# A four-layer convolution net on one core: new order numbers for the first layer, and half of the last tile's sums on another engine

## The chip, the cores and the metric

The kernel runs on one core of a Trainium2 chip, as one program. The metric is the device time in microseconds from the start of the program to its end on that core. The core's engines are TensorE (PE in the profile, its weight loads PEld), VectorE (DVE), ScalarE (ACT), GpSimd (POOL) and SyncE (SP, which here only issues transfers). Each takes its own instructions strictly in order and waits on semaphores for the others. Everything is computed in float32.

## The reference

Four layers are applied to x of shape 8 x 16 x 256 x 256. Each adds to x a function of the group-normalised x. The change lies in the first, a convolution with capsule routing over the eight images:

```python
votes = conv(gn(x), w)            # 3x3, 16 -> 128 channels = 8 atoms x 16
logits = 0
for _ in range(3):
    r = softmax(logits, axis=0)   # over the 8 images
    preds = squash(sum_over_atoms(votes * r))
    logits = logits + sum_over_channels(votes * preds)
x = x + preds
```

The other layers are a spline convolution, an attention over patches and a circular convolution. The change does not touch them.

## The kernel before

The first layer (`layer0`) works in 64 tiles of four image rows, `TILES = H // 4`. For one tile `work(i)` writes down the steps; none is emitted there. Each step is one call of `op` with its engine, an estimated time, a function that emits its instructions, and what it reads and writes. In the order of the list they are:

- `prepare` for the tile two further on: the load of the input (L478, SP), products L487 that take the mean out (PE), the move L490 (ACT), and the store L499 to a DRAM buffer (ACT queue).
- The votes, in two halves of two rows. The first half takes for each row one set of loads L528 (SP), eight small products L557 and eight L550 (PE) and two copies L572 into the votes buffer (ACT). The second half takes loads L610 and products L587 and L591 with copies L596.
- A squash: squares L641 (ACT), norm products L645 (PE), roots L659 to L661 (ACT), L665 and L666 (DVE), inverses L670 and L671 (ACT), L675 to L678 (POOL).
- Two rounds. Each has the factor products L697 (PE), a scaling L715 and two multiplications L723 (DVE) and the products L733 (PE) for each half; the copy L755 or L766 (ACT) and in the second round the sum L760 (POOL); the softmax over the images: transposes L780 (PE), maximum and difference L786 and L787 (DVE), exponential L792 (ACT), sum, reciprocal and share L796 to L798 (DVE), transposes back L804 (PE), copy L813 (ACT); and the weighted sum (`weighted`): products L831 (PE), products with the votes L842 (DVE, four for each half, into `dd` buffers) and five sums L851 (POOL) for each half. A squash follows.
- The end: factors L697 (PE), scalings L893 (DVE), the addition of x L896 (POOL, with the residual loaded by L884, SP), statistics L908 (ACT), and the stores L919 to L928 (SP).

`_Order` turns the list into one order for all engines. Each step has one number in the module's list `TIMES`, by its place counted from the end of the tile's list, and the step's rank is that number plus 48 for each tile:

```python
for m, o in enumerate(reversed(ops), 1):
    at = n * self.period + self.times[-m] if n else -1000.0 - m
    o.rank = (at, n, -m)
```

A heap then emits the step of smallest rank among those whose feeding steps have been emitted and for whose new buffers there is room. A step of a small or negative number is so emitted as soon as what feeds it has been. The buffers are counted by kind: `x=3` PSUM pairs (used by L487, the votes, the factors and the L831 of pairs of images), `u=2` PSUM banks, `v=6` votes, `dd=4` products, `io=1` for the input of L487 and the residual in turn, `pr=2` for L723. Several tiles are in work at once, their steps mixed on each engine, and the order in the steady part repeats from tile to tile.

Of the kernel before, what the change touches and what calls it, by code (L numbers as in the profile page):

```python
# [12 lines left out]
ALU = mybir.AluOpType  # L13
# [10 lines left out]
TILES = H // 4  # L24
# [160 lines left out]
class _Buf:  # L185
# [10 lines left out]


TIMES = [
    -1017.19, 743.46, 708.62, 498.18, -984.65, -996.51, -997.22, 751.01, 751.99, 751.01, 752.12, 750.77,
    -967.35, -903.62, -974.59, 753.99, 754.00, 753.77, 445.66, 393.73, -780.66, -960.80, 755.37, 755.59, 760.20,  # L200
    707.64, 775.69, 780.13, 782.25, 565.91, 658.76, 763.54, 681.24, 605.08, 709.84, 767.15, 644.09, 776.33,
    664.78, 790.04, 756.59, 796.59, 757.08, 765.74, 797.09, 318.31, 799.87, 800.80, 377.30, 696.72, 800.88,
    717.59, 571.56, 737.04, 802.63, 604.46, 530.71, 804.53, 784.88, 636.95, 657.50, 800.06, 517.07, 807.24,
    715.03, 742.15, 830.33, 840.65, 809.85, 812.29, 605.85, 802.98, 816.03, 807.95, 821.83, 824.88, 831.28,
    830.39, 840.66, 789.85, 845.72, 805.49, 748.11, 612.37, 736.06, 636.75, 809.44, 848.88, 838.39, 852.49,
    854.69, 850.98, 859.07, 855.18, 468.16, 857.49, 859.83, 859.02, 698.63, 610.89, 868.22, 704.59, 653.78,
    580.88, 884.00, 654.67, 695.12, 888.80, 889.83, 889.82, 808.47, 890.27, 690.66, 805.44, 696.48, 782.31,
    896.59, 899.53, 896.48, 777.07, 667.15, 682.59, 886.03, 640.00, 674.37, 898.75, 899.76, 887.82, 843.57,
    670.73, 902.64, 828.29, 828.95, 658.08, 885.55, 571.52, 801.95, -872.70, 907.37, 403.39, 814.67, 908.69,
    735.69, 919.60, 844.76, 829.08, -789.01  # L210
]


# [79 lines left out]
class _Net:  # L293
# [123 lines left out]
    def layer0(self, wd, bd, less0, tiles=range(TILES)):  # L417
# [5 lines left out]
        nc, tc = self.nc, self.tc  # L423
        xf = self.d["x"].rearrange("b c h w -> (b c) (h w)")
        last = B - 1
        with ExitStack() as st:
# [23 lines left out]
            for row in (0, H + 1):  # L450
                nc.sync.dma_start(
                    out=self.d0[row * ROW : row * ROW + ROW].rearrange("(p w) -> p w", p=P), in_=ring[0][:, 0, :]
                )
                nc.sync.dma_start(
                    out=self.x1[row and 15, :, :, row and 9, row and 1, :].rearrange("b c w -> (b c) w"),
# [3 lines left out]
                    out=self.x1p[:, row and 1, :, row and H // 2, :], in_=ring[0][:, 0, 0:W]  # L459
# [7 lines left out]
            def buf(kind, shape, name=None):  # L467
                pool = psum if kind in banks else sbuf
                n = {**places, **banks}[kind]
                return _Buf(kind, lambda: pool.tile(shape, F32, name=name or kind, tag=kind, bufs=n))  # L470
# [34 lines left out]
            def work(i):  # L505
# [3 lines left out]
                def op(*a, **k):  # L509
                    ops.append(order.op(*a, **k))  # L510
# [109 lines left out]
                def voted(h, a):  # L620
                    return [(v[h], a // 4, 0), (v[h], a // 4, 1)]
# [8 lines left out]
                def rows(ap):  # L630
                    return ap.rearrange("p (r w) -> p r w", w=W)
# [184 lines left out]
                def weighted(rs):  # L816


                    s = buf("s", [P, 2, 2, W])
                    for h in range(2):  # L820

                        def term(images, h=h):

                            rb = [buf("x", [P, 2, 512], "rb") if len(a) == 2 else buf("u", [P, 1, 512], "r6") for a in images]

                            def products():
                                for pair, r in zip(images, rb):
                                    for n, a in enumerate(pair):
                                        g, j = a // 4, (0, 2, 1, 3)[a % 4]
                                        at = slice(32 * j, 32 * j + 32)  # L830
                                        nc.tensor.matmul(  # L831
                                            r()[:, n], spread[at, g, h, :], rs()[at], start=True, stop=True
                                        )

                            op("PE", 1.25, products, [(rs, 0)], [(r, 0) for r in rb] + [(s, "turn")], mode="r32")
                            out = []
                            for pair, r in zip(images, rb):
                                n, a = len(pair), pair[0]
                                dd = buf("dd", [P, 2, 512])

                                def multiply(n=n, a=a, r=r, dd=dd):
                                    nc.vector.scalar_tensor_tensor(  # L842
                                        dd()[:, :n], r()[:, :n], 1.0 / B, v[h]()[:, a : a + n], ALU.subtract, ALU.mult
                                    )

                                op("DVE", 0.2 + 0.52 * n, multiply, [(r, 0)] + voted(h, a), [(dd, 0)])
                                out.append(dd)
                            return out

                        def add(out, a, b, us):  # L850
                            op("POOL", us, lambda: nc.gpsimd.tensor_tensor(out[0](), a[0](), b[0](), ALU.add),  # L851
                               a[1] + b[1], out[1])

                        d45, d6 = term([(4, 5), (6,)])
                        sh = (lambda h=h: s()[:, :, h], [(s, h)])
                        add(
                            sh,
                            (lambda h=h: rows(v[h]()[:, last]), voted(h, last)),
                            (lambda d=d6: rows(d()[:, 0]), [(d6, 0)]),
                            1.3,  # L860
                        )
                        d01, d23 = term([(0, 1), (2, 3)])
                        both = (d01, [(d01, 0)])
                        add(both, both, (d45, [(d45, 0)]), 2.4)
                        add(both, both, (d23, [(d23, 0)]), 2.4)
                        for n in range(2):
                            add(sh, sh, (lambda d=d01, n=n: rows(d()[:, n]), [(d01, 0)]), 1.3)
                    return s
# [941 lines left out]
```

## Time and profile before

| | us |
|---|---|
| median of 3 runs | 6244.17 |
| lowest, highest | 6235.46, 6245.69 |
| profiled execution | 6237.4 |
| its span, first to last instruction | 6235.3 |
| TensorE busy | 5930.8 (95%) |
| VectorE busy | 4895.1 (79%) |
| GpSimd busy | 3593.7 (58%) |
| ScalarE busy | 3073.6 (49%) |

The profile is of one execution. Its page gives each engine's busy time, the span in 40 equal slices of 156 us (a digit is the busy share in tenths), and groups of instructions by source line; the trace behind it answers by stretch of time, by wait and in order of time. L851 is line 851 of the kernel. A count such as x8 is of instructions on the chip, where a float32 product takes two. Times of matmuls overlap by a little, so that the distance from one start to the next is what counts.

### The profile page before, as it was taken

How to read it: one execution, taken by the hardware profiler on the slowest of the kernel's cores; microseconds unless marked ns; L12 is line 12 of the kernel's file. 1: busy time of each engine (PE TensorE's matmuls, PEld its weight loads, DVE VectorE, ACT ScalarE, POOL GpSimd, SP SyncE). 2: the span in 40 equal slices, each digit the busy share in tenths (PEclk: the TensorE clock that was granted, in tenths of full speed). 3: DMA queues.
4: the chain of work that ended last, by engine and by line, in shares of the span. 5: the costliest groups of instructions: out<-in, count | busy, mean ns of one | idle time of the engine just before them, and what ended most of it. 6: DMA issues, size and time to landing. Idle time of an engine off the chain costs nothing.

```text
span 6235.3 us, 111335 instructions
## 1 busy us (share of the span) xinstructions
PE 5930.8 (95%) x44488; PEld 2760.5 (44%) x44488; DVE 4895.1 (79%) x5771; ACT 3073.6 (49%) x4858; POOL 3593.7 (58%) x3040
## 2 busy tenths in 40 slices
PE   2999999999999999999968999999999999999998
PEld 0344444444444444444423444444444666666652
DVE  5799999999999999999968999999999433333321
ACT  0444544444454445444427888888888222111221
POOL 0588888888888888888873333434443111111123
PEclk9999999999999999999978999999999999999999
DMA  7455555555555555555516555555557443444358
GB/s 286 120 137 126 144 140 134 132 144 137 130 139 142 136 126 146 138 133 133 129 40 194 177 175 176 179 175 173 175 177 191 116 90 85 89 94 103 87 183 255
DMA packets 408790, 902.08 MB, mean 145 GB/s; under 512 B 62034, under 2 KB 195762, under 8 KB 364882
## 3 DMA queue, kind: packets, MB, share of 16 engines
q1 hardware_dynamic: 364434, 831.69, 48.8%
q10 hardware_dynamic: 33984, 34.08, 1.7%
q0 software_dynamic: 9856, 29.20, 1.7%
q8 instruction: 351, 5.75, 0.4%
q14 instruction: 165, 1.35, 0.1%
HBM read 684.09 MB, written 210.77 MB: 144 GB/s over the span
## 4 chain that ended last, share of the span: by engine, by line
PE 59%; DVE 26%; issue 7%; DMA 4%; POOL 3%; ACT 1%; SPq 0%; DVEq 0%; POOLq 0%; ACTq 0%
PE rb L831 8%; PE cv L587 7%; PE pqk L1535 7%; DVE bases L1089 7%; PE pl L733 6%; DVE e L1079 4%; PE cv L591 4%; PE po L1562 4%; PE cv L550 4%; PE pv L1542 4%; PE psc L1550 4%; PE p L1627 3%; DVE pr L723 2%; DVE a L1079 2%; DVE e L1058 2%
## 5 line engine op out<-in xcount | busy, mean ns | idle before, releaser
L1112 PE MATMUL ps<-bases,tw 128*32 128x512 f32 (+1 forms) x13824 | 1360.1, 546 | 16.5 <-POOL bases L1081 6.5
L851 POOL TENSOR_TENSOR dd<-dd 128x1024 f32<-128x1024 f32 x512 | 1210.9, 2365 | 70.9 <-DVE dd L842 65.6
L1081 POOL TENSOR_TENSOR bases<-e,a 128x1024 f32<-128x1024 f32 (+1 forms) x264 | 621.1, 2375 | 925.6 <-DVE e L1079 925.6
L723 DVE TENSOR_TENSOR pr<-v,fb 128x2048 f32<-128x2048 f32 (+1 forms) x512 | 1020.8, 2014 | 17.1 <-PE pl L733 12.6
L1112 PEld LDWEIGHTS ps<-bases,tw 128*32 128x32 f32 x13824 | 597.7, 109 | 800.3 <-issue 483.3
L842 DVE SCALAR_TENSOR_TENSOR dd<-rb,v 128x1024 f32<-128x1024 f32 x768 | 906.5, 1214 | 8.9 <-POOL dd L851 3.3
L851 POOL TENSOR_TENSOR s<-s,dd 128x512 f32<-128x512 f32 x512 | 647.0, 1274 | 15.1
L831 PE MATMUL rb<-rs,ct_fold 32*128 32x512 f32 x3072 | 592.9, 634 | 25.6 <-DVE pr L723 20.2
L1546 ACT ACTIVATE vt<-pv,w_b2v 128x128 f32<-128x128 f32 x512 | 146.1, 368 | 839.6 <-PE pv L1542 839.6
L733 PE MATMUL pl<-pr,ct_fold 128*32 128x512 f32 x3584 | 506.9, 603 | 4.3 <-DVE pr L723 4.3
L587 PE MATMUL cv<-kt,w 128*128 128x512 f32 x1024 | 497.2, 608 | 11.0 <-DMA kt<-d 9.8
L851 POOL TENSOR_TENSOR s<-v,dd 128x512 f32<-128x512 f32 x256 | 328.6, 1283 | 292.5 <-DVE dd L842 292.5
L1535 PE MATMUL pqk<-w_qk,t 128*128 128x512 f32 x1024 | 482.7, 594 | 4.6 <-POOL t L1529 4.6
L550 PE MATMUL cv<-kt,w 128*128 128x512 f32 x1024 | 477.4, 609 | 2.5 <-DMA kt<-d 2.5
L1567 DVE TENSOR_TENSOR y<-po,res 128x512 f32<-128x512 f32 x128 | 88.5, 691 | 490.1 <-PE po L1562 476.0
L1529 POOL TENSOR_TENSOR t<-t,emb 128x512 f32<-128x512 f32 x128 | 162.1, 1267 | 515.8 <-DVE t L1525 501.4
L1089 DVE SCALAR_TENSOR_TENSOR bases<-xr,xm,bases 128x1024 f32<-128x1024 f32 (+1 forms) x264 | 446.5, 1729 | 0.3 <-POOL bases L1081 0.3
L596 ACT COPY v<-cv 128x1024 f32<-128x1024 f32 x256 | 251.8, 1007 | 303.1 <-PE cv L591 303.1
L1066 ACT ACTIVATE sq<-a 128x1024 f32<-128x1024 f32 (+1 forms) x264 | 263.8, 999 | 230.2 <-DVE a L1058 229.5
L831 PEld LDWEIGHTS rb<-rs,ct_fold 32*128 32x128 f32 x3072 | 226.1, 185 | 325.5 <-issue 129.3
L697 PEld LDWEIGHTS fb<-f,ct_fold 64*128 64x128 f32 x3072 | 208.7, 188 | 310.5 <-issue 177.0
L842 DVE SCALAR_TENSOR_TENSOR dd<-r,v 128x512 f32<-128x512 f32 x256 | 176.9, 691 | 190.8 <-PE r L831 176.3
(281 smaller groups left out, 10164.7 us busy)
## 6 DMA issues: line engine op xcount, KB each, us to landing
xr<-x1p SPq DMA_DIRECT2D x120, 1024.0 KB
kt<-d SPq DMA_DIRECT2D x256, 387.0 KB
kt<-d SPq DMA_DIRECT2D x128, 516.0 KB
d<-dn ACTq DMA_DIRECT2D x64, 516.0 KB
kr<-d SPq DMA_DIRECT2D x128, 258.0 KB
kt<-d SPq DMA_DIRECT2D x128, 258.0 KB
x<-y SPq DMA_DIRECT2D x128, 258.0 KB
xs<-in_x_dram SPq DMA_DIRECT2D x16, 2048.0 KB
```

The source lines that it names most:

```text
L550: nc.tensor.matmul(ps[g]()[:, n], w[:, 0], t[:, a : a + 2, 0:W], start=False, stop=True)
L587: nc.tensor.matmul(ps()[:, n], w2[:, 0, j, :], t[:, a : a + 2, 0:W], start=True, stop=False)
L723: nc.vector.tensor_tensor(pr()[:, :n].rearrange("p n (r w) -> p n r w", w=W), v[h]()[:, 4 * g : 4 * g + n].rearrange("p n (r w) -> p n r w ...
L733: nc.tensor.matmul(pl()[at : at + 32], sel[:, g, h, :], pr()[:, t, :], start=h == 0 and g == 0, stop=h == 1 and (g == 1 or t == 3),)
L831: nc.tensor.matmul(r()[:, n], spread[at, g, h, :], rs()[at], start=True, stop=True)
L842: nc.vector.scalar_tensor_tensor(dd()[:, :n], r()[:, :n], 1.0 / B, v[h]()[:, a : a + n], ALU.subtract, ALU.mult)
L851: op("POOL", us, lambda: nc.gpsimd.tensor_tensor(out[0](), a[0](), b[0](), ALU.add), a[1] + b[1], out[1])
L1079: nc.vector.tensor_tensor(q, q, part[4 + k], ALU.mult)
L1081: nc.gpsimd.tensor_tensor(ring[n % 3][:, 0, p : p + m, 1 : 1 + W], rows(e), rows(a), ALU.subtract)
L1089: nc.vector.scalar_tensor_tensor(r, rows(part[1]), xm[:, b : b + 1], v, ALU.is_gt, ALU.mult)
L1112: nc.tensor.matmul(out if k is None else out[:, k], lhs, rhs, start=start, stop=stop, skip_group_check=True)
L1535: nc.tensor.matmul(ps, t[:, n, k * P : (k + 1) * P], wqk[:, n, :], start=n == 0, stop=n == 1)
```

## The change

All 149 numbers of `TIMES` are replaced. The period of 48, the lists of steps, their buffers and what feeds what stay. Besides, in `weighted`, the function `add` takes its engine from outside: for the second half (`h` = 1) of the last tile (`i` = 63) the five sums of each round go to VectorE, `nc.vector.tensor_tensor` in place of `nc.gpsimd.tensor_tensor`. All others stay on GpSimd.

```diff
--- before.py
+++ after.py
@@ -196,18 +196,19 @@
 
 
 TIMES = [
-    -1017.19, 743.46, 708.62, 498.18, -984.65, -996.51, -997.22, 751.01, 751.99, 751.01, 752.12, 750.77,
-    -967.35, -903.62, -974.59, 753.99, 754.00, 753.77, 445.66, 393.73, -780.66, -960.80, 755.37, 755.59, 760.20,
-    707.64, 775.69, 780.13, 782.25, 565.91, 658.76, 763.54, 681.24, 605.08, 709.84, 767.15, 644.09, 776.33,
-    664.78, 790.04, 756.59, 796.59, 757.08, 765.74, 797.09, 318.31, 799.87, 800.80, 377.30, 696.72, 800.88,
-    717.59, 571.56, 737.04, 802.63, 604.46, 530.71, 804.53, 784.88, 636.95, 657.50, 800.06, 517.07, 807.24,
-    715.03, 742.15, 830.33, 840.65, 809.85, 812.29, 605.85, 802.98, 816.03, 807.95, 821.83, 824.88, 831.28,
-    830.39, 840.66, 789.85, 845.72, 805.49, 748.11, 612.37, 736.06, 636.75, 809.44, 848.88, 838.39, 852.49,
-    854.69, 850.98, 859.07, 855.18, 468.16, 857.49, 859.83, 859.02, 698.63, 610.89, 868.22, 704.59, 653.78,
-    580.88, 884.00, 654.67, 695.12, 888.80, 889.83, 889.82, 808.47, 890.27, 690.66, 805.44, 696.48, 782.31,
-    896.59, 899.53, 896.48, 777.07, 667.15, 682.59, 886.03, 640.00, 674.37, 898.75, 899.76, 887.82, 843.57,
-    670.73, 902.64, 828.29, 828.95, 658.08, 885.55, 571.52, 801.95, -872.70, 907.37, 403.39, 814.67, 908.69,
-    735.69, 919.60, 844.76, 829.08, -789.01
+    -241.80, 1267.36, 967.15, 1267.78, -317.12, -9592.42, -9510.80, 1237.73, 1244.26, 1244.40, 1189.33, 1179.12,
+    -411.35, -9592.40, -9565.99, 1247.56, 1247.54, 1247.55, 1127.18, 1050.73, -9570.40, -9417.31, 1249.49,
+    1225.65, 1258.37, 1194.66, 1272.62, 1204.40, 1275.43, 1128.46, 1155.43, 1267.32, 1155.75, 1186.63, 1134.96,
+    1158.05, 1252.16, 1272.85, 1257.73, 1047.50, 1282.74, 1285.57, 1285.59, 1287.82, 1291.47, 905.73, 1252.61,
+    1294.01, 1292.82, 1234.61, 1144.78, 1295.16, 837.55, 1072.04, 1247.71, 1296.90, 882.08, 1298.35, 1301.08,
+    1301.07, 1278.03, 1113.28, 1302.33, 1303.94, 1270.90, 1045.97, 1272.85, 1321.07, 1312.22, 1013.34, 949.41,
+    1101.94, 1187.26, 1069.24, 1228.20, 1319.61, 1321.06, 1286.61, 1324.53, 978.08, 1335.17, 1245.21, 1301.69,
+    1009.77, 1336.18, 1182.73, 1240.39, 1342.35, 1262.73, 1347.48, 1290.73, 1343.30, 1359.45, 1350.46, 973.22,
+    1353.21, 1290.53, 1357.82, 1363.20, 1204.10, 1363.46, 1087.12, 1135.69, 1120.04, 1368.85, 1369.65, 915.34,
+    1381.08, 1381.83, 1381.72, 1336.02, 1346.39, 1383.59, 1384.17, 1021.12, 1342.69, 1388.71, 1385.12, 1389.76,
+    1148.16, 1385.21, 1142.08, 1324.94, 982.89, 1304.57, 1247.67, 1265.42, 1275.31, 1322.68, 1399.86, 1314.82,
+    1401.07, 1309.13, 1236.24, 1407.41, 1181.29, 1336.78, -81.98, 1413.37, 1232.44, 1427.09, 1417.19, 1273.86,
+    1429.04, 1436.16, 1442.32, -9595.18
 ]
 
 
@@ -847,8 +848,10 @@
                                 out.append(dd)
                             return out
 
-                        def add(out, a, b, us):
-                            op("POOL", us, lambda: nc.gpsimd.tensor_tensor(out[0](), a[0](), b[0](), ALU.add),
+                        name, engine = ("DVE", nc.vector) if h and i == TILES - 1 else ("POOL", nc.gpsimd)
+
+                        def add(out, a, b, us, name=name, engine=engine):
+                            op(name, us, lambda: engine.tensor_tensor(out[0](), a[0](), b[0](), ALU.add),
                                a[1] + b[1], out[1])
 
                         d45, d6 = term([(4, 5), (6,)])
```

Some of the numbers, by step, as they stand in the two lists (a step that comes after its feeders takes its real place from theirs where that is later):

| step | old | new |
|---|---|---|
| L487, products of `prepare` | 743.46 | 1267.36 |
| L557, first votes | 751.01 | 1237.73 |
| L697, first round, second half | 797.09 | 1291.47 |
| L831, first round, second half, first and second piece | 809.85, 816.03 | 1312.22, 1187.26 |
| L760, sum of the second round | 868.22 | 1363.46 |
| L780, transpose of the second round | 704.59 | 1087.12 |
| L831, second round, second half, first piece | 896.48 | 1389.76 |
| L697, end of the tile, two halves | 907.37, 908.69 | 1413.37, 1417.19 |

## Prediction

> **What bounds the kernel now.** I read the page's slices first, then the steady part of the first layer by stretches, then what TensorE waits for there, and last the end of that layer in order of time.
>
> ```profile
> PE   2999999999999999999968999999999999999998
> DVE  5799999999999999999968999999999433333321
> POOL 0588888888888888888873333434443111111123
> ```
>
> The first layer fills slices 1 to 20 and both parts of the change lie in it. TensorE and VectorE are at 9 all the way; the dip in slice 20 is the drain into the second layer. Busy time by stretches, the first row being one tile of the steady part:
>
> ```profile
> core 0: us, PE busy (x) PEld busy (x) DVE busy (x) ACT busy (x) POOL busy (x), PEclk, DMA share, GB/s
> 1003.39:1050.98 47.59, 46.90 (x293) 19.39 (x293) 43.37 (x47) 23.43 (x45) 42.09 (x36) 1.00 0.54 137
> ...
> 3243.80:3276.80 33.00, 11.15 (x60) 5.07 (x60) 10.40 (x12) 5.31 (x14) 20.80 (x16) 0.55 0.15 42
> ```
>
> One tile takes 47.59 us and TensorE is busy 46.90 of it. An order can't take work away, so with the same matmuls it can win the idle 0.69 us and little else; what it can lose has no such bound. The last row is the end of the last tile: TensorE 11.15 of 33 us, GpSimd 20.80. There the work is one chain. TensorE's own waits between 1000 and 3000 us:
>
> ```profile
> PE lg L780 <- POOL ls L760: 13.5, 42, 0.3
> PE rb L831 <- DVE pr L723: 13.4, 42, 0.4
> ```
>
> 42 tiles, two waits of 0.32 us in each: the transpose of the second round's logits waits for GpSimd's sum L760, and the second-half products of the second round wait for VectorE's multiplication L723, which still reads the PSUM buffer that they want.
>
> **The new order.** A step's number plus 48 per tile gives its place, and a step can't come before those that feed it; so its place is the larger of its own number and of theirs. Sorted within one period, the old numbers give just the TensorE order of the timeline (transpose L780, votes, factor L697, votes, L804, L487, products L831 and so on). I sorted the new ones in the same way, counted from the second-round transpose at 0. Most of the order stays. What moves on TensorE: the products L487 of a coming tile go from 19.2 (behind L804) to 47.9, the last thing ahead of the transpose; the two factors L697 of the tile's end go from 39.2 and 40.5 to 1.9 and 5.7 of the next period; the second-half products of the first round, split until now, come in one piece; the first votes' L557 come ahead of the factor L697 of the first round's second half instead of behind it. VectorE's and GpSimd's ends of the tile (L893, L896) move along.
>
> **Steady part, term by term.** (1) *The wait at L780.* From the end of the last L733 to the transpose the trace has 2.19 us (1048.79 to 1050.98: copy, sum L760, signals). TensorE fills 1.87 of it with a factor (0.65) and eight L831 (1.22). The new order fills it with one L645 (0.46 to 0.58) and L487 (1.82): 2.28 or more. The wait of 0.32 goes. What is late next is L760's own chain, 0.1 us behind.
> (2) *Factors side by side.* One end factor comes to stand beside the first round's factor, without the change to another kind of matmul between them. Changes cost little here: the same factor takes 0.54 to 0.77 us by what follows. I take -0.03, bounds -0.15 and +0.15.
> (3) *The wait at L831.* VectorE gets one scaling of 0.69 us (L893) between the softmax's share and L723; the other fills the 0.71 us in which it waited for ScalarE's exp. Before, L723 of the first half ended 0.86 us after the first L831 began (1013.34 against 1012.48). TensorE now has 0.5 + 2.97 us (L804, votes) from the share to L831 and VectorE 0.69 x 2 + 3.95, so L723 ends some 1.6 us after. Then VectorE needs 4.09 (L842), 0.5 (L665, L666), 0.7 (L715), 3.95 (L723), so 11.0 us from L831 to L831 where the trace has 10.50; and since L557 (1.08) is now ahead of the factor that L715 needs, up to 0.5 more. If the second-half L831 still take the buffer that L723 holds, this costs 0.5 to 1.0 us in each tile. But in the old order that buffer, of three, was the first handed out of those in use (factor, then two votes); in the new one the votes are handed out ahead of the factor, so the next in turn is a vote's, which ScalarE frees with a copy of 1.01 us. If that is the copy of the first votes, it ends while the second votes (1.8) run, and costs nothing; if it is that of the second, it costs 1.15 us. I take 0, bounds -0.32 and +1.15, since L831 at 1012.48 did start before L723 had freed its buffer, so another was then at hand.
> (4) *Transfers.* L487's input had 6.06 us from issue (1004.60) to use (1010.66) and made no steady wait; it now has some 30. The residual of the same size shares the one buffer and now has over 10 us in place of 36, more than those 6.06. L487's move L490 and its store L499 come a quarter of a period later, with 17 us until the next votes' fetch L610. That fetch (issued 1022.69, used 1033.59) stands on SP behind the six stores of a tile (1005.00 to 1009.78), which move some 9 us later, to about 13 to 18: still clear, by 3 us. I take 0; past that cover it costs what the stores overrun.
> Sum: -0.32 - 0.03 = -0.35 us per tile. The steady part lasts from 216.65 to 3153, 61.7 tiles: -22 us. Bounds by the terms: -0.79 (-49 us) and +0.98 (+60 us).
>
> **The last tile.** GpSimd's sums of the second round, with nothing else beside them:
>
> ```profile
> 3246.70 1.27 POOL L851 TENSOR_TENSOR s<-v,dd 128x512 f32<-128x512 f32 x1 [8.51 <-DVE dd L842]
> 3248.97 4.77 POOL L851 TENSOR_TENSOR dd<-dd 128x1024 f32<-128x1024 f32 x2 [1.00 <-DVE dd L842]
> 3253.69 1.27 POOL L851 TENSOR_TENSOR s<-v,dd 128x512 f32<-128x512 f32 x1
> 3254.91 1.26 POOL L851 TENSOR_TENSOR s<-s,dd 128x512 f32<-128x512 f32 x1
> 3256.14 2.33 POOL L851 TENSOR_TENSOR dd<-dd 128x1024 f32<-128x1024 f32 x1
> 3258.44 1.26 POOL L851 TENSOR_TENSOR s<-s,dd 128x512 f32<-128x512 f32 x1
> 3259.66 2.34 POOL L851 TENSOR_TENSOR dd<-dd 128x1024 f32<-128x1024 f32 x1
> 3262.07 2.60 POOL L851 TENSOR_TENSOR s<-s,dd 128x512 f32<-128x512 f32 x2
> ```
>
> Both halves' ten sums run one behind the other until 3264.7. Half of them is 2 x 2.37 + 1.28 + 2 x 1.27 = 8.56 us. VectorE's nearest rows for such a sum are 1.21 us (L1079, 128x1024) and 0.69 (L798, 128x512), though each has one operand in PSUM: 2 x 1.21 + 3 x 0.69 = 4.49. Both ends for the pair: side by side, GpSimd's half ends at 3256.2 and VectorE's, held by its own L842 and by free dd buffers, at 3258.6, 6.1 us sooner; one at a time 8.56 + 4.49 = 13.05 in place of 17.1, 4.1 us sooner. I take 4.1, for this row: VectorE's L1089, which reads two operands from SBUF, begins while GpSimd adds in the second layer.
>
> ```profile
> 3501.33 2.31 DVE L1089 SCALAR_TENSOR_TENSOR bases<-xr,xm,bases 128x1024 f32<-128x1024 f32 x1
> ...
> 3504.33 1.28 DVE L1089 SCALAR_TENSOR_TENSOR bases<-xr,xm,bases 128x1024 f32<-128x1024 f32 x1
> ```
>
> The first begins 1.2 us before GpSimd's second L1081 ends (3502.55) and takes 2.31; the second, with GpSimd idle, takes 1.28. Of the overlap of 1.2 us, 1.03 is lost.
>
> [...]
>
> In the first round the last tile's sums lie among the tile before's and TensorE's factors. There the new order also puts L733 and L697 ahead of the L645 that waits for the tile before (old: L645 at 3225.55, L733 behind it, until 3234.9). With the factor done early the pieces behind L645 are L733 twice and one L723, 4.4 us less. GpSimd's L760 no longer stands behind an L896 (1.2). Against it, VectorE's sums lie in the softmax of the tile before. Together 4.1 + 4.4 + 1.2 = 9.7; I take -10, bounds 0 and -16 (with 6.1 in both rounds and the 4.4).
>
> Profiled execution: 6237.4 (span 6235.3 and 2.1 around it) - 22 - 10 = **6205 us**. It lies 6.8 below the median of the three runs, 6244.17, and 2 above the lowest; I make no correction for that.
>
> **The rivals.**
> A, the forecast: 6205, between 6185 (the L831 wait goes too and the end gives 16) and 6222. For it: the wait at L780 has its cover, and TensorE is the only engine that is full.
> B, one wait for another: the 0.35 won at L780 comes back at L831, where VectorE is later. Steady part unchanged, only the end is shorter: 6227. For it: VectorE's chain of 11.0 us against 10.50. Against it: the buffers' turn.
> C, slower: TensorE stands before the second-half L831, for L723's or the second vote copy's buffer, 0.5 to 1.15 us in each tile. It decides from +0.6 us, where the 0.35 and the end are used up (0.25 x 61.7 = 15, against 10). At 0.95, 0.60 net x 61.7 = 37, less 10: 6264; with 1.15 and term 2's upper bound 6288. Against it: VectorE idles 4.2 us in a tile and could make up what it lost.
> D, the change doesn't do what it says: VectorE's sums push back what GpSimd and the softmax of the tile before do, and the steady order is as good as the old one: 6237.
>
> **Chances.** A 0.45, B 0.17, C 0.28, D 0.10. What a measurement of this kernel can tell from no change is some 0.2%, 12.5 us. Faster by over that: A, and half of B (6227 lies beside the bound of 6225): 0.53. Within: the other half and D: 0.19. Slower: C, 0.28. The range runs from A's low end, 6185, to 6290, C's upper end.
>
> **What would show it.** Right: a tile of 47.2 us in the steady part, no TensorE wait at L780, at L831 no more than 0.4 us; L851 on VectorE in ten instructions of the last tile, and some 10 us less from 3153 to the last store. Wrong: a tile of 47.6 or more; a wait at L831 of 0.5 us or more, released by L723 or by ScalarE's L572; waits for transfers L610 or L884; VectorE's L851 at twice their lone length beside GpSimd's with no shorter end.

## The result, and the profile after

| | before | after |
|---|---|---|
| median, us | 6244.93 (6235.46 to 6246.46, 4 runs) | 6541.49 (6531.49 to 6574.28, 4 runs) |
| profiled execution; its span | 6237.4; 6235.3 | 6531.49; 6529.6 |
| one tile of the steady part | 47.59 | 49 to 57, on average 52.5 (47.59 + 300.65 / 61.7, from the next row) |
| last votes' end to the first store of the last tile | 3151.19 to 3274.28: 123.1 | 3451.84 to 3564.47: 112.6 |

The ratio after to before is 1.0491 (95% interval 1.046 to 1.0522). The forecast was 6205, with a range up to 6290: the kernel became 4.9% slower, far outside of it. One execution of run 5 below took 18062.85 us; nothing here says why, and the ratio given there leaves it out.

In the changed file the lines of the first layer stand one to three further on: L587 is now L588, L610 is L611, L780 is L781, L831 is L832, L842 is L843, L851 is L854, the stores L919 to L928 are L922 to L931. In kernels with added lines they move again by three to six.

The slices of the page, 163 us each:

```profile
PE   2999999999999989999995999999999999999998
...
DVE  5788888888888778888887999999999633333331
...
POOL 0688888777887777878786434344433211111123
```

The first layer now fills 22 slices instead of 20. VectorE and GpSimd fell from 9 and 8 to 8 and 7: they wait more. TensorE still shows 9, which hides what happened, since a slice that is 92% busy is a 9 too, and since a slow matmul counts as busy (the wide votes took 686 ns on average, 608 before). The group of the wide votes says it (busy us, mean ns of one, idle us just before them and what ended it):

```profile
L588 PE MATMUL cv<-kt,w 128*128 128x512 f32 x1024 | 571.9, 686 | 223.5 <-DMA kt<-d 222.4
```

Before, the same group was busy 497.2 us with 11.0 us of idle time ahead of it. So 212.5 us more of waiting for a fetch, and 74.7 us more for the very same matmuls. The votes behind them, L592, add 19.7 (290.0 to 309.7). Together 307, of which everything else gives back some 13: the span grew by 294.3.

TensorE's waits between 1000 and 3000 us (sum, times, longest):

```profile
PE cv L588 <- DMA kt<-d: 146.5, 37, 7.1
PE lg L781 <- DVE dd L843: 25.5, 38, 0.7
```

Neither of the two old waits is there any more. In their place stands one of 4.0 us on average in 37 of 38 tiles, for the second half's votes input, and a new one of 0.67 at the transpose of the first round. One slow tile by stretches, the columns as in the prediction:

```profile
2062.79:2117.49 54.70, 48.69 (x293) 19.47 (x292) 43.54 (x47) 23.38 (x44) 42.24 (x36) 0.94 0.48 119
```

The same 293 matmul records took 48.69 us instead of 46.90, at a mean granted clock of 0.94 instead of 1.00, and 6.0 us went idle.

Why the fetch is late is to be read in SyncE's issues of one tile, in order of time (start, length of the issue):

```profile
1502.42 0.38 SPq L922 DMA_DIRECT2D x<-s  x1
1502.85 0.66 SPq L923 DMA_DIRECT2D x1p<-s  x1
1503.55 0.47 SPq L922 DMA_DIRECT2D x<-s  x1
1504.07 0.61 SPq L923 DMA_DIRECT2D x1p<-s  x1
1504.72 1.35 SPq L929 DMA_DIRECT2D x<-s  x1
1506.12 1.96 SPq L479 DMA_DIRECT2D xs<-in_x_dram  x1
1508.17 0.57 SPq L529 DMA_DIRECT2D kr<-d  x1
1508.85 1.16 SPq L611 DMA_DIRECT2D kt<-d  x2
```

By the sizes on the page (256 KB four times, 128 KB, and 512 KB for the input) 1.1 MB of stores and 0.5 MB of input stand right ahead of the fetch, besides the 258 KB of `kr`, a load for the first votes (L529), which stands ahead of it in the other kernels here too. The fetch is issued in good time, at 1508.85, and TensorE reaches its votes at 1519.6:

```profile
1519.02 0.60 PE L805 MATMUL rt<-ct_fold,e 128*128 128x128 f32 x4
1523.22 1.96 PE L588 MATMUL cv<-kt,w 128*128 128x512 f32 x4 [3.60 <-DMA kt<-d]
```

From issue to first use are 14.4 us. Before, they were 10.9 us with no wait (1022.69 to 1033.59), and the stores stood 13 to 18 us ahead of it.

The trace also keeps the updates of the semaphores by which a transfer reports, so the landing itself can be read: it is the last update for the fetch's two transfers. Between 1000 and 3000 us the fetch landed 7.6 us after its issue in before (median; 7.1 to 10.1) and 14.3 us after it in after (12.1 to 17.4). When the fetch was issued in before, `kr` alone was still under way on SyncE's queue, that is, without its last update. In after it was `kr`, stores of 0.4 MB and the input of 0.5 MB, in every tile (the sizes are those of whole transfers, of which a part may have moved by then). TensorE was ready for the data 10.9 us after the issue in before and 10.5 in after (medians). So there was a cover of some 3 us, and the fetch came 6.6 us later.

### The profile page after: what moved, and what is told of

The parts are those of the page before. It is cut to its first block, busy times and chain, and to the rows that moved or that the text cites. A ratio compares the mean times of both kernels' runs of the same rounds, so it can differ in the third digit from the quotient of the medians.

```text
span 6529.6 us, 111447 instructions
## 1 busy us (share of the span) xinstructions
PE 6010.2 (92%) x44488; PEld 2753.2 (42%) x44488; DVE 4916.0 (75%) x5781; ACT 3071.7 (47%) x4858; POOL 3592.1 (55%) x3030
## 4 chain that ended last, share of the span: by engine, by line
PE 60%; DVE 20%; DMA 15%; issue 3%; POOL 1%; ACT 1%; SPq 0%; POOLq 0%; DVEq 0%; ACTq 0%
DMA kt<-d 12%; PE cv L588 8%; PE rb L832 7%; PE pqk L1538 7%; DVE bases L1092 6%; PE pl L734 6%; PE cv L592 4%; DVE e L1082 4%; PE po L1565 4%; PE cv L551 4%; PE psc L1553 3%; PE pv L1545 3%; PE p L1630 3%; PE fb L698 3%; DVE a L1082 2%
## 5 line engine op out<-in xcount | busy, mean ns | idle before, releaser
L854 POOL TENSOR_TENSOR dd<-dd 128x1024 f32<-128x1024 f32 x508 | 1201.5, 2365 | 37.8 <-DVE dd L843 22.8
L843 DVE SCALAR_TENSOR_TENSOR dd<-rb,v 128x1024 f32<-128x1024 f32 x768 | 904.7, 1217 | 15.3 <-POOL s L854 1.5
L588 PE MATMUL cv<-kt,w 128*128 128x512 f32 x1024 | 571.9, 686 | 223.5 <-DMA kt<-d 222.4
L854 POOL TENSOR_TENSOR s<-s,dd 128x512 f32<-128x512 f32 x508 | 645.6, 1282 | 25.0
L854 POOL TENSOR_TENSOR s<-v,dd 128x512 f32<-128x512 f32 x254 | 325.2, 1280 | 602.5 <-ACT sq L911 514.9
L832 PE MATMUL rb<-rs,ct_fold 32*128 32x512 f32 x3072 | 594.8, 639 | 8.1 <-DVE pr L724 3.5
L1549 ACT ACTIVATE vt<-pv,w_b2v 128x128 f32<-128x128 f32 x512 | 146.5, 369 | 840.6 <-PE pv L1545 808.5
L734 PE MATMUL pl<-pr,ct_fold 128*32 128x512 f32 x3584 | 520.3, 605 | 11.1 <-DVE pr L724 10.8
L843 DVE SCALAR_TENSOR_TENSOR dd<-r,v 128x512 f32<-128x512 f32 x256 | 175.9, 687 | 420.7 <-PE r L832 410.5
L551 PE MATMUL cv<-kt,w 128*128 128x512 f32 x1024 | 473.7, 605 | 0.0
L832 PEld LDWEIGHTS rb<-rs,ct_fold 32*128 32x128 f32 x3072 | 205.8, 186 | 392.5 <-issue 163.8
L588 PEld LDWEIGHTS cv<-kt,w 128*128 128x128 f32 x1024 | 192.8, 209 | 403.6 <-issue 373.6
```

Source lines behind the costliest of these rows:

```text
L551: nc.tensor.matmul(ps[g]()[:, n], w[:, 0], t[:, a : a + 2, 0:W], start=False, stop=True)
L588: nc.tensor.matmul(ps()[:, n], w2[:, 0, j, :], t[:, a : a + 2, 0:W], start=True, stop=False)
L734: nc.tensor.matmul(pl()[at : at + 32], sel[:, g, h, :], pr()[:, t, :], start=h == 0 and g == 0, stop=h == 1 and (g == 1 or t == 3),)
L832: nc.tensor.matmul(r()[:, n], spread[at, g, h, :], rs()[at], start=True, stop=True)
L843: nc.vector.scalar_tensor_tensor(dd()[:, :n], r()[:, :n], 1.0 / B, v[h]()[:, a : a + n], ALU.subtract, ALU.mult)
L854: op(name, us, lambda: engine.tensor_tensor(out[0](), a[0](), b[0](), ALU.add), a[1] + b[1], out[1])
```

## The experiments

Theory **T** after this reading: the place of the stores alone loses the time. The store step's number, -9595.18, means "as soon as its data is there"; the additions L899 that feed it moved within the period, and the stores with them, right ahead of the fetch. Rivals: the new order of the engines is itself slower (**E**), or VectorE's sums in the last tile cost something (**S**). All runs compute the whole reference. Landings are medians from 1000 to 3000 us, with the lowest and the highest. Times are medians; ratios are to the kernel before on the same chip.

**1. Stores later, nothing else** (store_later).

```diff
+TIMES[-1] = 1437.0
```

> The changed kernel with one number moved: the tile's six stores (1.1 MB) are issued just behind the fetch L611 for the second-half votes, no longer just ahead of it. The input of L488 (0.5 MB) stays ahead. Theory T, transfers: TensorE's 3.7 us wait at L588 in each tile is for that fetch, which stands behind the stores and the input; with the stores gone from ahead of it most of the wait goes, and so does the slow start of L588: 6220 to 6300 us, the wait at L588 under 1 us per tile. Rival P, the PSUM buffers and VectorE's order (the prediction's case C) are what stretches the tile and the wait for the fetch only hides it: another wait of 3 us or more turns up at L832, 6450 us or more. Rival S, TensorE's order alone is dearer: 6500 us.

Measured: 6213.62 (6204.91 to 6217.88), ratio 0.9961 (0.9946 to 0.9977). TensorE's waits from 1000 to 3000 us and one tile:

```profile
PE lg L784 <- DVE dd L846: 28.2, 42, 0.7
```

```profile
2059.26:2106.51 47.25, 46.53 (x293) 18.82 (x293) 43.55 (x47) 23.39 (x44) 42.20 (x36) 1.00 0.52 138
```

One number out of 149 moves the time by 328 us. The wait for the fetch is gone, the clock is back at 1.00, a tile takes 47.25, and the time is a little below the 6220 to 6300 of the expectation. SyncE now issues the fetch first (L614 at 1534.06) and the stores right behind it (1535.24 to 1539.8); the fetch lands after 7.4 us (6.9 to 8.7). T holds and E falls: the engines' order is the changed kernel's.

**2. Stores, input and residual later** (both_later).

```diff
+TIMES[-1] = 1437.0
+TIMES[0] = 1245.2
+TIMES[137] = 1411.5
```

> The changed kernel with three numbers moved: the stores, then the input of L488, are issued behind the fetch L611, and the residual's load stays behind L488. Theory T: nothing large stands ahead of the fetch, as in the order before; no wait at L588, a tile of 47.2 to 47.6 us, 6205 to 6235 us. If the input alone still costs something in the run with only the stores moved, this one is the faster by it. Rival P: a wait at L832 of 0.5 to 1.2 us per tile is left, 6265 to 6310. Rival S: 6500.

Measured: 6207.79 (6201.37 to 6214.64), ratio 0.995 (0.9936 to 0.9963). The tile is 47.25 again, the wait of 0.67 at the transpose is unchanged. Once the stores are behind the fetch, the input's place is worth nothing that the time can tell (the two intervals overlap).

**3. The old order with the stores put close to the fetch** (old_store_close): the kernel before, with

```diff
+TIMES[-1] = 942.3
```

> The kernel before with one number moved: the tile's stores are issued just ahead of the fetch L610 for the second-half votes instead of some 14 us before it. Everything TensorE, VectorE, ScalarE and GpSimd do keeps its order. Theory T: the order before becomes slow by the same wait; 2 to 4 us of wait at L587 per tile, 6370 to 6500 us. Rivals P and S: the order of the engines is unchanged, 6235 to 6250.

Measured: 6398.25, ratio 1.0255 (1.0238 to 1.0272).

```profile
PE cv L590 <- DMA kt<-d: 72.4, 33, 5.5
PE rb L834 <- DVE pr L726: 12.8, 40, 0.4
PE lg L783 <- POOL ls L763: 12.6, 39, 0.3
PE cv L590 <- ACT rs L816: 8.4, 5, 1.9
PE cv L590 <- issue: 4.6, 2, 2.4
```

The two old waits still stand, since the engines' order is the old one, and beside them the same wait for the fetch. The last two rows are that fetch too: in all 40 tiles the votes begin within 0.14 us of its landing. So some half of the loss (158 of 297 us) can be given to the old order with one number, and the loss taken from the new one with one: T from both sides. The wait is smaller here (85.4 us in 40 tiles, 2.1 each). The stores are issued at 1503.38 to 1507.2, behind the residual (0.5 MB), and the fetch at 1514.04; by then the residual has landed, and 0.4 MB of the stores are still under way, without an input. The fetch lands after 11.5 us (10.4 to 14.6).

**4. The old order with VectorE's sums** (old_order_dve_sums): the changed kernel with the old list of numbers.

> The old numbers, with only the second part of the change: VectorE makes the second half's sums in the last tile. The prediction's term: two operations by turns save 4.1 us in the second round and up to as much in the first, 6227 to 6237 against 6237 of the profiled execution (0.997 to 1.000). If the two engines could run side by side: 6 us in each round, 6225. If VectorE's sums hold up the softmax of the tile before: 6237 or more.

Measured: 6241.24, ratio 1.0002 (0.9994 to 1.0011). The sums alone win nothing. The reason lies in the round before the last. There VectorE's sums (now L853) go into the middle of the softmax of the tile before:

```profile
3198.15 1.22 DVE L842 SCALAR_TENSOR_TENSOR dd<-rb,v 128x1024 f32<-128x1024 f32 x1
3199.28 2.48 DVE L853 TENSOR_TENSOR dd<-dd 128x1024 f32<-128x1024 f32 x2
3201.79 0.69 DVE L853 TENSOR_TENSOR s<-s,dd 128x512 f32<-128x512 f32 x1
3202.40 0.68 DVE L796 TENSOR_REDUCE e<-lg 128x64 f32<-128x512 f32 x1
```

In the kernel before, L796 followed L842 directly, at 3198.31. It is 4.1 us later here, and so are the products L842 behind it (3208.54 against 3204.45). In the second round the sums then win about 2.9 us: from the first product to the last sum 15.9 us (3250.05 to 3265.96) instead of 18.8 (3245.93 to 3264.7). From the last votes to the first store it takes 124.7 us instead of 123.1.

**5. The new order, stores later, all sums on GpSimd** (store_later_pool_sums): the kernel before with the new list, and

```diff
+TIMES[-1] = 1437.0
```

> The new numbers with the stores moved behind the fetch, and all sums back on GpSimd: what is left of the second part of the change in the new order. With the stores moved and VectorE's sums the median was 6213.6. If those sums save 4 us in each of two rounds or at least in the last: 6217 to 6224. If they give back in the softmax of the tile before what they save, as in the old order: 6211 to 6216. The end of the layer, from the last votes to the last stores, tells it better than the time.

Measured: 6214.76, ratio 0.996 (0.9947 to 0.9974), against 6213.62 for run 1. The end is 114.5 us long, against 112.6 in run 1. So in the new order VectorE's sums are worth 2 us of the profile, which the times can't tell from nothing. In the second round itself, from the first product to the last sum, they save 3.8 us: 15.3 (3218.29 to 3233.60 in run 1) against 19.1 (3221.81 to 3240.91 here). Ahead of that round they cost 1.8: from the last votes to its first product it takes 87.7 us in run 1 and 85.8 here. S falls too: the sums explain none of the loss, and next to none of the gain.

**6. Stores from GpSimd's queue** (store_gpsimd_queue): the changed kernel, with every store issued by GpSimd behind its additions.

```diff
-nc.sync.dma_start(out=place(...), in_=t()...)
+nc.gpsimd.dma_start(out=place(...), in_=t()...)
-op("SP", 2.0, store, ...)
+op("POOL", 2.0, store, ...)
```

> The changed kernel with the tile's stores issued from GpSimd's queue at the same moment, right behind its last sum L899; the fetch L611 keeps its place. If the fetch is late because it stands in one queue behind the stores (theory T1), it now overtakes them: 6210 to 6260 and no wait at L588 above 1 us, less what five issues on GpSimd cost it. If it is late because both move over the same transfer engines (theory T2), the wait stays: 6400 to 6540.

Measured: 6548.68, ratio 1.0498 (1.0484 to 1.0512). As a test of the time it is a miss. The wait at L588 is gone, but the time is as bad as after's, for another reason: the five issues take 3.4 us in GpSimd's order (1516.45 to 1519.8), its sums come later, and TensorE waits elsewhere.

```profile
PE lg L781 <- DVE dd L843: 101.2, 38, 2.7
PE fb L698 <- POOL f L679: 47.2, 37, 1.4
```

The time and the missing wait say nothing on the fetch, since TensorE came to its votes later as well (16.7 us after the issue). The landing does: 10.5 us after the issue (9.2 to 12.2). So with the stores under way on another queue, and the input landed, the fetch came later than in before (7.6), and earlier than with the stores on its own queue (12.6, run 9).

**7. Half of the stores ahead** (half_ahead): the store step cut in two; the two stores of the first half (0.5 MB) keep their number, the rest goes to 1437.0. Ahead of the fetch 0.5 MB of stores and 0.5 MB of input are issued.

> The changed kernel with the store step cut in two: the first half's two stores (0.5 MB) stay ahead of the fetch L611, the second half's three or four (0.6 MB) go behind it. Theory T: the wait follows the bytes that stand ahead. The changed kernel has 1.6 MB ahead (stores 1.1, input 0.5) and waits 3.7 us, the one with all stores moved has 0.5 and waits 0. With 1.0 MB ahead the wait is between, 0 to 2 us per tile: 6210 to 6350. If instead any store ahead brings the whole wait: 6500.

Measured: 6215.06 (6211.46 to 6218.07), ratio 0.9962 (0.9949 to 0.9976), with no wait at the votes. The fetch was issued at 1535.33 and used at 1546.35, 11.0 us later. It landed after 9.7 us (9.2 to 10.7), 2.1 later than in before but still inside the cover. When it was issued, the input and `kr` were still under way, and nearly always none of the stores.

**8. The input behind the fetch, stores ahead** (input_later).

```diff
+TIMES[0] = 1245.2
```

> The kernel after with one number changed: the input fetch of L479 (0.5 MB) moves from right behind the stores to 1245.2 us (the period is 1491.5), behind the fetch of L611; the six stores (1.1 MB) stay ahead of the fetch. Known so far: 1.6 MB ahead cost about 4.8 us per tile, 1.0 MB (half of the stores, and the input) ahead cost nothing. If it is the bytes ahead that count, 1.1 MB is hardly more than 1.0: wait at L588 below 20 us in 1000 to 3000 us, time 6205 to 6240. If it is the stores as such (their writes to the device's memory, or their many small packets), the wait stays above 70 us and the time is 6380 to 6540.

Measured: 7889.54, ratio 1.2645 (1.2624 to 1.2666). A miss, and not on the question. (The period of the order is 48, not the 1491.5 of the expectation.) Input and residual share the one `io` buffer and take it by turns. With the input's number above the residual's, residuals took it tile after tile: SyncE issues L890 `res` at 1510.27, 1557.79 and 1591.97 and no input until 1622.69.

```profile
1629.93 3.75 PE L491 MATMUL pd<-xs,wd 128*128 128x512 f32 x4 [13.37 <-DMA xs<-in_x_dram]
1657.79 3.75 PE L591 MATMUL cv<-kt,w 128*128 128x512 f32 x4 [24.11 <-DMA kt<-d]
```

Until then the tiles in work run dry, and then the next ones start from nothing. A list of numbers can lose 26% by one buffer's turn; run 2 had moved the residual along, and lost nothing.

**9. The same with the residual moved along** (stores_ahead_alone).

```diff
+TIMES[0] = 1245.2
+TIMES[137] = 1411.5
```

> The kernel after with two numbers changed: the input (L479's fetch, 1245.2) and the residual (L887's, 1411.5) go to the places they have in both_later, in their old order to each other; the stores stay ahead of L611's fetch. So 1.1 MB of stores alone stand ahead of it. If the bytes ahead count, 1.1 MB is hardly more than the 1.0 MB of half_ahead: wait at L588 below 20 us in 1000 to 3000 us, 6205 to 6240. If the stores as such make it late, or the margin lies just between 1.0 and 1.1 MB, the wait stays above 40 us and the time is 6300 to 6540.

Measured: 6339.18 (6336.75 to 6348.94), ratio 1.0168 (1.0151 to 1.0185).

```profile
PE cv L592 <- DMA kt<-d: 67.4, 37, 4.4
PE lg L785 <- DVE dd L847: 27.6, 41, 0.7
PE cv L592 <- ACT rs L818: 4.5, 4, 1.2
```

With the stores' 1.1 MB alone ahead, TensorE still waits 1.8 us on average for the fetch (72.0 us in 41 tiles; the last row is the fetch too, as the votes begin 0.14 us behind its landing there). Issued at 1544.20, it is used at 1557.31, 13.1 us later. Time and wait are those of the second expectation, which had two readings: the stores as such, or a margin between 1.0 and 1.1 MB. The landings speak for the first. The fetch lands after 12.6 us (11.4 to 14.4) here and after 9.7 in run 7. The stretch in which the bytes ahead were issued is alike (6.2 us here, 6.0 there) and there are 0.1 MB more, but the fetch lands 2.9 us later; the 0.5 MB of input that after has ahead of it besides add only 1.6 (14.3 against 12.6). So in these runs the stores weighed more than a load of the same size; why was not tested.

**10. The fetch from ScalarE's queue** (fetch_act_queue): the changed kernel, only L611 issued elsewhere, behind the same 1.6 MB.

```diff
-                            nc.sync.dma_start(
+                            nc.scalar.dma_start(
```

> The kernel after with one edit: the wide fetch of L611 (two transfers of 516 KB a tile) is issued from ScalarE's queue instead of SyncE's, at the same place of the order; the stores and the input stay on SyncE's queue where after has them. Two readings of why the fetch lands 14 us after its issue. If the transfers of one queue are served in order and the fetch stands behind the bytes of the stores: it starts at once in a queue of its own, the wait of TensorE at L588 for kt (146.5 us in 1000 to 3000 us) goes or falls below 20, and the time is 6205 to 6240. If the transfer engines are shared by the packets of all that is under way: the wait stays at 100 us or more, 6450 to 6560. Between, 6280 to 6420, if the fetch gets a share of the engines beside the stores: both are then true in part. The stores themselves land later in the first reading, and nobody waits for them.

Measured: 6273.2 (6269.89 to 6284.74), ratio 1.0061 (1.0046 to 1.0076).

```profile
PE rb L832 <- DVE dd L843: 7.4, 41, 0.5
PE cv L588 <- ACT rs L814: 3.6, 3, 1.2
PE cv L588 <- DMA kt<-d: 2.3, 7, 0.5
PE cv L588 <- ACT v L573: 1.4, 2, 0.7
PE cv L588 <- issue: 1.2, 3, 0.6
```

All four rows at L588 are the fetch: in all 15 tiles the votes begin within 0.14 us of its landing. The wait for it falls from 146.5 to 8.5 us, although the stores and the input are under way on SyncE's queue as before. The fetch lands 11.5 us after its issue (10.1 to 13.0), and TensorE comes for it after 11.7 us, 1.2 later than in after. So of the 6.6 us by which the fetch came later in after than in before (14.3 against 7.6), 2.8 go on ScalarE's queue, and 3.8 stay beside the same traffic. Both readings of the expectation are true in part: the 2.8 us belong to the place in SyncE's queue; the second, transfer engines shared by all that is under way, would take the 3.8 us, and no run shows it by itself. The time, 6273, lies just outside the range for that case, between it and the first one. The queue change is not free: ScalarE spends 1.98 us on the two issues, the copy L573 behind them begins 2.67 us after the one ahead of them ends (0.65 in after), and the second-half products L832 come in two pieces. A tile takes 48.3 us on average, not 47.25.

**11. The remaining wait taken away** (d6_first): run 2, and VectorE's product L843 for the single image in the second round's second half gets a number that makes it early, as in the old order.

```diff
+TIMES[-1] = 1437.0
+TIMES[0] = 1245.2
+TIMES[137] = 1411.5
+TIMES[120] = 900.0
```

> The numbers of the run with stores and input moved, and one more: in the second round's second half VectorE takes the product with the single image (L842 of 128x512) ahead of the three pairs, as in the order before, not after them. That frees the one-bank PSUM buffer for the first round's transpose, for which TensorE waits 0.67 us in each tile. If that wait goes and none comes: a tile of 46.6 us, 40 us less, 6165 to 6175. If another takes its place (VectorE's chain into the second-half L831, or the copies): 6195 to 6210.

Measured: 6194.31 (6189.42 to 6200.05), ratio 0.9929 (0.9917 to 0.9942); faster than before and after, and by its tile than run 2 (the intervals of the two ratios just overlap). TensorE shows no wait at all between 1000 and 3000 us, and a tile takes 46.97. Only 0.28 of the 0.67 us was won. The half of the tile that held the wait is shorter by 0.62 (23.97 to 23.35), the other longer by 0.34 (23.28 to 23.62), nearly all of it in the first votes just behind the transpose:

```profile
2047.36 0.66 PE L787 MATMUL lg<-ct_fold,ls 128*128 128x128 f32 x4
2047.95 1.28 PE L564 MATMUL cv<-kr,w 32*128 32x512 f32 x8
2049.16 3.70 PE L557 MATMUL cv<-kt,w 128*128 128x512 f32 x8
2052.83 0.63 PE L811 MATMUL rt<-ct_fold,e 128*128 128x128 f32 x4
```

From the transpose to L811 it takes 5.47 us here and 5.17 in run 2, where TensorE had stood still for 0.67 us just ahead of it. In before, with no pause there either, the same stretch takes 5.61 (1027.52 to 1033.13). Why the blocks are shorter behind the pause was not settled.

## Why the prediction was wrong

The step that failed is **(4) Transfers**, and in it the price of the fetch: "still clear, by 3 us … I take 0; past that cover it costs what the stores overrun". The 3 us asked whether SyncE's *issues* of the stores end before the fetch is issued. They did (in after the stores' issues end at 1506.07, the fetch's begins at 1508.85). But an issue is no transfer: the fetch joined a queue in which 1.6 MB had been issued in the 6.4 us before it (1502.42 to 1508.85) and transfers of 0.9 MB of that were still under way. The term had a place and a gap but no bytes, so no bound on it ever stood in the range. It also left out that the input, which had been issued ahead of the stores, would come between them and the fetch. (A tile has five stores, not the six of the prediction.) What it had to ask is when the fetch lands: 7.6 us after its issue in before, with `kr` alone under way ahead of it, and 14.3 in after. That is 6.6 us more against a cover of some 3: TensorE was ready for the data 10.9 us after the issue in before and 10.5 in after. What was left over is the wait of 4.0 us a tile. Of the 6.6 us, 2.8 are the place in SyncE's queue, since they go when the fetch is issued from ScalarE's queue (run 10); the other 3.8 stay beside the same traffic, and their cause is open.

The second part of the loss was in no step. In after, TensorE doesn't only stand still, it comes back slowly. The wide votes of another tile, and the granted clock around them (the third column from the end, by stretches):

```profile
1576.41 3.51 PE L588 MATMUL cv<-kt,w 128*128 128x512 f32 x4 [5.70 <-DMA kt<-d]
```

```profile
1572.00:1576.40 4.40, 0.00 (x0) 0.03 (x1) 1.60 (x1) 0.00 (x0) 0.44 (x1) 0.97 1.01 201
1576.40:1578.00 1.60, 1.59 (x2) 0.81 (x3) 0.00 (x0) 0.00 (x0) 0.00 (x0) 0.50 0.31 88
1578.00:1580.00 2.00, 2.00 (x5) 0.49 (x5) 0.00 (x0) 0.00 (x0) 0.00 (x0) 0.62 0.26 98
1580.00:1582.00 2.00, 2.00 (x12) 0.77 (x14) 0.00 (x0) 0.92 (x2) 0.00 (x0) 1.00 0.12 45
```

After these 5.70 us without work the clock is 0.50, and four of these matmuls take 3.51 us instead of 1.9. Over the layer that is the 74.7 + 19.7 us of the two vote groups, nearly a third of the loss.

The other steps, one by one:

- **(1) The wait at L780** went, and 0.32 us with it: no row for it in after or in run 1. But a wait of 0.67 us appeared where the prediction had not looked, at the transpose of the *first* round (L781, released by VectorE's L843), until then one of the places without a wait.
- **(2) Factors side by side**: right in its direction, too small in size. TensorE's busy time in a tile fell from 46.90 to 46.53 (run 1), ten times the 0.03 taken and beyond its bound of 0.15. From the start of each block to the next start, less idle time, the six blocks of factors took 3.89 us in before and 3.64 in run 1 (means of 40 tiles): 0.25 less, so the step was too small by itself. The first votes L550 and L557 gave another 0.40, and the other blocks took back some 0.27. That this comes from the changes between kinds of matmul was not tested.
- **(3) The wait at L831**: no such wait, so rival C's mechanism isn't there. The 0.32 us of L723's wait went as well, the lower bound rather than the 0.
- **Sum** -0.35: run 1 gives 47.25 - 47.59 = -0.34 a tile, and 20.6 us less up to the last votes (3130.63 against 3151.19) where -22 was forecast. The sum is right and its terms are not: -0.32 - 0.32 - 0.37 + 0.67.
- **The last tile** -10: measured 10.5 (123.1 to 112.6). Again the sum and not the terms. In the second round the two engines save 3.8 us, close to the 4.1, but ahead of it VectorE's sums cost 1.8, which the sum named and did not count; 2 us are left (runs 1 and 5). The new order saves the other 8.6 (114.5 with all sums on GpSimd, against 123.1), where 5.6 was taken.
- **Rival D** named one thing rightly: in the old order VectorE's sums push back the softmax of the tile before, by 4.1 us (run 4); in the new order they cost the 1.8 us just named.

A's low end, 6185, is also 5 us above what its own terms give (6237.4 - 0.67 x 61.7 - 16 = 6180).

With the stores' number mended the profiled execution takes 6204.91 us (median 6213.62), where 6205 was forecast for it. That agreement is luck in part, since several terms were off and cancelled. What sank the change was a step that was taken at nothing without asking for its bytes.

## What to carry to other kernels

When a reordering moves a store, or what feeds a store that goes "as soon as it can", ask which fetch is issued next, how much is then still under way, on its own queue and on others (2.8 and 3.8 of the 6.6 us here), and how long it has from its landing to its reader; a gap between issues is no cover (it was 2.78 us here, and TensorE waited 4.0 us a tile). A fetch with a reader waiting goes ahead of stores that nobody waits for; here that is one number and 328 us. And a wait of some microseconds on TensorE is priced with the slow start behind it (94.4 us here, beside 212.5 of waiting).

## What the runs showed of the hardware

**The fetch landed later behind stores, and also beside them.** The same fetch of 2 x 516 KB, from its issue to its landing, and TensorE's wait for it, both from 1000 to 3000 us:

| kernel | still under way at its issue, besides `kr` (258 KB) | issue to landing, us: median (lowest to highest) | wait at the votes, us |
|---|---|---|---|
| store_later | nearly always nothing | 7.4 (6.9 to 8.7) | none |
| before | nothing on its queue | 7.6 (7.1 to 10.1) | none |
| half_ahead | 0.5 MB of input | 9.7 (9.2 to 10.7) | none |
| store_gpsimd_queue | stores, on GpSimd's queue | 10.5 (9.2 to 12.2) | none |
| old_store_close | 0.4 MB of stores | 11.5 (10.4 to 14.6) | 85.4 |
| fetch_act_queue | as in after, but on SyncE's queue while the fetch is on ScalarE's | 11.5 (10.1 to 13.0) | 8.5 |
| stores_ahead_alone | 0.4 MB of stores, in some tiles 0.6 | 12.6 (11.4 to 14.4) | 72.0 |
| after | 0.4 MB of stores, 0.5 MB of input | 14.3 (12.1 to 17.4) | 146.5 |

**The slow start did not follow the length of the pause alone.** Of the 22 waits at L588 from 1000 to 2200 us in after, 5 were followed by four matmuls in 1.96 us (after pauses of 1.78 to 3.64 us) and 17 by 2.44 to 3.75 us (after 2.09 to 7.13). A pause of 2.37 gave 3.17, one of 3.60 gave 1.96. The half clock is in the rows (0.50). In this trace's record of the granted clock it comes in 17 stretches between 1000 and 2200 us, one at each slow start. They last 3.41 or 6.83 us and begin whole multiples of 3.41 us apart. Where a pause fell on this raster counted beside its length: pauses of 3.31 and 3.37 us that began 1.1 and 0.9 us behind one of its steps were each followed by four matmuls in 3.75 us, pauses of 3.13, 3.60 and 3.64 us that began 1.5 us behind one by four in 1.96.

**VectorE and GpSimd held each other up on sums from SBUF.** In after's last tile, VectorE's first sum of 128x1024 begins while GpSimd ends a sum of its own, and GpSimd's two small sums then lie beside the end of that one and beside VectorE's second:

```profile
3542.57 4.78 POOL L854 TENSOR_TENSOR dd<-dd 128x1024 f32<-128x1024 f32 x2 [1.00 <-DVE dd L843]
3547.42 4.52 POOL L854 TENSOR_TENSOR s<-s,dd 128x512 f32<-128x512 f32 x2
```

```profile
3546.65 1.77 DVE L854 TENSOR_TENSOR dd<-dd 128x1024 f32<-128x1024 f32 x1
...
3549.59 1.23 DVE L854 TENSOR_TENSOR dd<-dd 128x1024 f32<-128x1024 f32 x1
```

VectorE's first sum takes 0.54 us more than its second (1.77 against 1.23), and 0.70 us of it lie beside GpSimd's (3546.65 to 3547.35). GpSimd's two small sums take 4.52 us, where the prediction's row of before has 2.60 for two with VectorE's sums absent. So where the two engines overlapped, most of the overlap was lost (0.54 of 0.70 us on VectorE; on GpSimd 1.92 of the 2.23 us beside VectorE's two sums), as the prediction's row of L1089 had it; the saving in this round was 3.8 us, near the 4.1 of strict turns and not the 6.1 of working side by side.
